# Layer 2 of a four-layer network: centring behind the relu's additions, one half's residual behind the next turn's factor products, one product instruction a half

## The chip, the cores and the metric

The kernel runs on one core of a Trainium2 chip. The metric is the time of one execution in microseconds (us) on the device. A core has five engines with a queue each, which run in order and wait for one another through semaphores: PE (TensorE, matrix products and transposes), DVE (VectorE), ACT (ScalarE), POOL (GpSimd) and SP (SyncE, which here issues every DMA). PE writes into PSUM[...].

## The reference, cut to what matters

Four layers are added to the image one after the other; each works on a group normalisation of its input. The change lies in the stretch in which the end of layer 1 and the whole of layer 2 are computed, with the first statistics of layer 3.

```
x = x + L1(gn(x))        # its last step: relu of a normalised product of the input and a factor per pixel
x = x + L2(gn(x))
x = x + L3(gn(x))

def L2(x):                                     # "involution", 3 x 3
    r  = relu(batchnorm(x @ Wr))               # 256 -> 64 channels
    w  = (r @ Ws).reshape(B, H, W, 16, 1, 9)   # nine weights for each of 16 groups, per pixel
    xi = x @ Wi                                # 256 -> 256
    patches = nine shifts of padded xi, stacked, reshaped to (B, H, W, 16, 16, 9)
    return sum(w * patches, axis=-1)
```

There are 16 images of 64 x 64 pixels and 256 channels, all in float32.

## The kernel before, in words

Layer 2 is the second of three blocks of the program. An image is cut into 8 chunks of 512 pixels. One loop of 151 turns does four jobs a turn, each on its own chunk, at distances given by `LAG`: `end` (the end of layer 1), 12 turns later `proj` (the projection xi of the same chunk), 20 turns later `inv` (the involution), and 30 turns later `cen` (the centring of the finished chunk for layer 3). In a steady turn the four jobs are in up to four images. The order of instructions on each engine is the order in which the code is written (`tc.manual_schedule()`).

The jobs, with their lines and the names of their tiles:

- `end_of_layer1` (L965) is a generator in three parts. First DVE makes `z` and `pf`, one for each half of the channels, from `x1` and the factors (L975). Then ACT applies the relu to both (L981) and POOL adds `x1`, which gives `x2` (L985). Last ACT squares `x2` for statistics (L992).
- `projected` (L1031): PE computes `px` for two halves, eight matmuls (L1038), ACT writes them into the padded image `pad` (L1042) and, at an image's last chunk, copies two edge columns (L1049, L1050).
- The involution needs `prepare` one turn ahead: `reduced2` gives `pr` and, through ACT, `rt` (L1059, L1062); `weights` gives `pw`, once for each half (L1069); `patches` transposes `pad` into `pt`, and ACT copies nine of them into `xs` (L1084, L1088). Then `products` (L1107) multiplies patches by weights on DVE, into `pd`, in four instructions a half, one for each row of pixels. Half 0 is summed over its nine taps on POOL (`sums_on_pool`, L1122 and L1123), half 1 on DVE (L1258). Both go into `x3`. `residual` (L1093) transposes `x2` into two PSUM tiles `lo`, and DVE adds one to each half of `x3` (L1261): half 1 first, then half 0, which has to wait for POOL.
- `turned` (L1125), a turn later, transposes `x3` into `c3`; `statistics3` (L1152) squares it. `stores` collects DMAs, which SP issues at the start of the next turn.
- `centred` (L1174): POOL subtracts the mean `gmb` from a loaded chunk `xc` (L880), and twelve DMAs write the result into `strips`.

Norms run beside this as generators, `norm2` and `norm3`: moments (L113 to L123), a matmul (`pg`), copies of the group mean (L140, and L142 for `ngm2`), the deviation (L146 to L148), a matmul (`pv`; with it `pb`, L864, in `norm3`), then `isq` (L93) and for `norm3` a copy of `pb` into `gmb` (L869). `norm2` ends with small matmuls `pm` (L1020) from which DVE makes `b2` and `bis` (L1026, L1028). Each call of `step()` moves every running norm by one part. A turn has three: one behind `turned` (before `projected`), one behind both products, and one at the end. A norm's first part (the moments) is run at the start of the turn after the statistics are complete.

A turn is called by r, its number modulo 8. In r=3 the next involution begins a new image, and `prepare` has to come behind `projected`, which writes the last chunk of that image; in all other turns it comes ahead of the relu. `norm3` computes its moments at r=5, its matmuls `pv` and `pb` and its `isq` at r=6. `norm2` computes its moments at r=0, `isq` at r=1, `bis` at r=3.

PSUM tiles: `pt`, `pr`, `px`, `pg`, `pv`, `pb` and `pm` all come from one pool, "tr", of three buffers. A new tile waits until the reader of the tile that had its buffer is done. Which of the three buffers a tile gets is settled when the program is built. `lo` has a pool of two buffers, `pw` one of three, `pd` and `xs` two each.

Of the kernel before, what the change touches and what calls it, by code (L numbers as in the profile page):

```python
# [11 lines left out]
ALU = mybir.AluOpType  # L12
# [3 lines left out]
P = 128  # L16
C = 256
# [19 lines left out]
def network(ctx: ExitStack, tc: tile.TileContext, a: dict, out: bass.AP):  # L37
    nc = tc.nc
# [59 lines left out]
    def step():  # L98

        for c in list(chains):  # L100
            if next(c, c) is c:
                chains.remove(c)
# [77 lines left out]
    with ExitStack() as st:  # L180
# [366 lines left out]
        def loads(n):  # L547
            for job in jobs(n):
                if job[0] == "q":
                    load("xn", job[1], job[3])  # L550
                else:
                    load(*job)
# [78 lines left out]
    with ExitStack() as st:  # L631
# [57 lines left out]
        for n in range(10):  # L689
            delta, c = n // 2, n % 2  # L690
# [28 lines left out]
        with tc.manual_schedule():  # L719
# [25 lines left out]
            for n, (ch, g) in enumerate(steps):  # L745
# [18 lines left out]
                b, k = g * 8, min(8, NI - g * 8)  # L764
# [134 lines left out]
    with ExitStack() as st:  # L899
# [45 lines left out]
        def taken(name):  # L945

            n = [k for k, _ in loaded].index(name)
            return loaded.pop(n)[1]
# [11 lines left out]
        def load_centred(i, rc):  # L960
            load("xc", [P, 4, C], *(
                (lambda t, k=k: t[:, k], src) for k, src in enumerate(centred_from(i, rc))
            ))

        def end_of_layer1(i, rc):  # L965

            if rc == 0:
                st0[i] = [
                    wk.tile([P, 2, NCH], F32, tag=f"st0{k}", name="st0") for k in range(2)
                ]  # L970
            sums, squares = st0[i]
            x1, pf = taken("x1"), taken("pf")
            zs = [wk.tile([P, 2, 256], F32, tag="z", name="z", bufs=1), pf]
            for h, z in enumerate(zs):
                nc.vector.scalar_tensor_tensor(  # L975
                    z, x1[:, h], ngm1[:, i, h : h + 1], pf, ALU.add, ALU.mult
                )
            yield
            x2 = wk.tile([P, 2, CT], F32, tag="x2", name="x2")
            for h, z in enumerate(zs):  # L980
                nc.scalar.activation(  # L981
                    z, z, AF.Relu, bias=bnp[:, 1, h : h + 1], scale=ab[:, 0, i, h : h + 1],
                    accum_out=sums[:, h, rc : rc + 1],
                )
                nc.gpsimd.tensor_tensor(  # L985
                    x2[:, h].rearrange("p (t g) -> p g t", g=2), z, x1[:, h], ALU.add
                )
            stores.append((x2_d[i, rc], x2))
            yield
            sq = wk.tile([P, CT], F32, tag="sq", name="sq", bufs=1)  # L990
            for h in range(2):
                nc.scalar.activation(  # L992
                    sq, x2[:, h], AF.Square,
                    bias=ngm1[:, i, h : h + 1], accum_out=squares[:, h, rc : rc + 1],
                )
            if rc == NCH - 1:
                begun.append(norm2(i))
# [104 lines left out]

        def products(oh, pw, xs):
            pd = pd_p.tile([P, 4, P, 9], F32, tag="pd", name="pd")
            for r in range(4):
                run = xs[:, r : r + 3].rearrange("p e j c -> p (e j c)")
                nc.vector.tensor_tensor(  # L1107
                    pd[:, r].rearrange("p (g f) k -> p g f k", f=16),
                    run[:, oh * 9 * P : (oh + 1) * 9 * P].rearrange(
                        "p (g f k) -> p g f k", f=16, k=9  # L1110
                    ),
                    pw[:, r].rearrange("p (g k) -> p g k", k=9).unsqueeze(2).broadcast_to(
                        [P, 8, 16, 9]
                    ),
                    ALU.mult,
                )
            return pd

        def sums_on_pool(pd, x3):
# [5 lines left out]
        def turned(i, rc, x3):  # L1125

            if rc == 0:
                st3[i] = [
                    wk.tile([P, 2, NCH], F32, tag=f"st3{k}", name="st3") for k in range(2)
                ]  # L1130
            c3 = wk.tile([P, 2, 2, 256], F32, tag="c3", name="c3", bufs=2)
            for oh in range(2):
                pt = tr.tile([P, 4, P], F32, tag="tr", name="pt")
                for r in range(4):
                    nc.tensor.transpose(pt[:, r, :], x3[:, r, oh * P : (oh + 1) * P], ident)
                nc.scalar.activation(  # L1136
                    c3[:, oh], pt.rearrange("p r t -> p (r t)").rearrange("p (t g) -> p g t", g=2),
                    AF.Copy, accum_out=st3[i][0][:, oh, rc : rc + 1],
                )
            x3n = x3_d[i].rearrange("(g r w) c -> g w r c", g=2, w=HW)  # L1140
            for g in range(2):
                stores.append((x3n[g][:, rc * 4 : rc * 4 + 4], x3[g:P:2]))
            for h in range(2):
                stores.append((
                    c3_d[i, :, h].rearrange("p (g t) -> p g t", g=2)[
                        :, :, rc * 256 : rc * 256 + 256
                    ],
                    c3[:, h],
                ))
            return c3  # L1150
# [23 lines left out]
        def centred(i, rc):  # L1174
            cen = wk.tile([P, 4, 4, 64], F32, tag="cen", name="cen")
            stores.extend(centred_strips(i, rc, taken("xc"), cen, gmb[i]))
# [6 lines left out]

        LAG = (0, 12, 20, 30)
        TURNS = NI * NCH + 23

        def jobs(n):

            at = [divmod(n - lag, NCH) for lag in LAG]
            return [
# [13 lines left out]
        with tc.manual_schedule():  # L1206
            loads(0)
            ahead, made = None, None
            for n in range(TURNS):
                end, proj, inv, cen = jobs(n)  # L1210
                nxt = jobs(n + 1)[2]
                done, stores[:] = list(stores), []
                loads(n + 1)
                for dst, src in done:
                    nc.sync.dma_start(out=dst, in_=src)
                nxt_cen = jobs(n + 1)[3]
                if nxt_cen:
                    load_centred(*nxt_cen)
                now, ahead = ahead, None
                for c in begun:  # L1220
                    next(c)
                chains.extend(begun)
                begun.clear()
                ending = end_of_layer1(*end) if end else None
                if ending:
                    next(ending)
                if inv:
                    w1 = weights(now[1], 1)
                    x3 = wk.tile([P, 4, C], F32, tag="x3", name="x3", bufs=3)

                def prepare():
                    x2r, rt = reduced2(*nxt)
                    ahead = [x2r, rt]
                    ahead.append(patches(*nxt, lambda: ahead.append(weights(rt, 0))))
                    return ahead

                if nxt and nxt[1]:
                    ahead = prepare()
                if ending:
                    next(ending)  # L1240
                if inv:
                    los = residual(now[0])
                c3 = turned(*made) if made else None
                step()
                if proj:
                    projected(*proj)
                if inv:
                    pd = products(0, now[2], now[3])
                    sums_on_pool(pd, x3)
                if nxt and not nxt[1]:  # L1250
                    ahead = prepare()
                if inv:
                    pd1 = products(1, w1, now[3])
                step()
                if made:
                    statistics3(*made[:2], c3)
                if inv:
                    nc.vector.tensor_reduce(x3[:, :, P:C], pd1, AX.X, ALU.add)  # L1258
                    for oh in (1, 0):
                        half = x3[:, :, oh * P : (oh + 1) * P]  # L1260
                        nc.vector.tensor_tensor(half, half, los[oh], ALU.add)  # L1261
                step()
                if ending:
                    next(ending, None)
                made = (*inv, x3) if inv else None
                if cen:
                    centred(*cen)
            for dst, src in stores:
                nc.sync.dma_start(out=dst, in_=src)

# [2 lines left out]
    with ExitStack() as st:  # L1273
# [203 lines left out]
        for n, (i, quarter, t) in enumerate(turns):  # L1477
# [41 lines left out]
            if n % gap == 2 and n // gap < NCH:  # L1519
                cen = wk.tile([P, 4, 4, 64], F32, tag="xw", name="cen", bufs=6)  # L1520
# [3 lines left out]
            if n in features:  # L1524
                tp, k = features[n]
# [124 lines left out]
```

## Time and profile before

| | |
|---|---|
| time, median of 3 runs | 8560.48 us (8559.8 to 8580.07) |
| the profiled execution: time, span | 8603.53 us, 8601.7 us |
| layer 2's products, first to last start | 3634.3 to 6178.6 us |
| DVE busy from 4100 to 5834 us | 1638 of 1734 us |
| POOL, ACT, PE busy in the same stretch | 1253, 1075 and 1311 us |
| DMA engines busy in the same stretch | 0.71 of 16 engines, 233 GB/s |

The profile's page lists the busy time of each engine, its share in 40 equal slices of the span, and groups of instructions by source line with their number, busy time, mean duration in ns, and the idle time just before them with what ended it. The timeline gives single instructions in order: start, duration, engine, line, operation, output<-inputs, and in brackets the idle time before and its end. A mean over a group can hide two kinds of turn, and a busy engine can be stalled inside an instruction.

### The profile page before, as it was taken

To read this page: it belongs to the slowest core of one execution; us is meant where nothing else is said; L and a number is where in the kernel's file an instruction comes from. 1 tells how busy PE (TensorE), PEld (TensorE's weight loads), DVE (VectorE), ACT (ScalarE), POOL (GpSimd) and SP (SyncE) were. 2 spreads that over 40 slices of the span, in tenths; PEclk is the share of its full clock that TensorE was granted. 3 is DMA by queue.
4 is the path that set the end of the run, shared out by engine and by line. 5 is a ranking of instruction groups with operands and counts; after the bars stand their busy time and mean duration, and the time that the engine had idled before them with its cause. 6 is when DMAs were issued, how large, how long until landed. Compare 5 with 4: busy or idle time off the path is not lost. (4 is left out here: it accounts for less than half of the span.)

```text
span 8601.7 us, 215728 instructions
## 1 busy us (share of the span) xinstructions
PE 6924.3 (80%) x88348; PEld 5146.2 (60%) x88348; DVE 6022.7 (70%) x7839; ACT 4835.8 (56%) x11136; POOL 3054.3 (36%) x2154
## 2 busy tenths in 40 slices
PE   7888888888888776477777777778588888888888
PEld 5666666666666542254555555555376767777776
DVE  6777777777766757499999999999744444444444
ACT  3555555555555536666666656665355555555554
POOL 1222222222222200367777777777611112111112
PEclk9999999999999868799888888889799999999999
DMA  6543333443333327756767677676578878888887
GB/s 221 180 141 133 133 128 133 142 137 130 130 113 108 101 80 244 234 188 230 241 230 239 229 232 236 228 240 195 173 222 257 248 243 255 252 258 252 252 256 241
DMA packets 1081775, 1695.70 MB, mean 197 GB/s; under 512 B 138834, under 2 KB 684963, under 8 KB 1079635
## 3 DMA queue, kind: packets, MB, share of 16 engines
q1 hardware_dynamic: 1080786, 1681.90, 60.7%
q8 instruction: 696, 11.40, 0.6%
q14 instruction: 293, 2.39, 0.1%
HBM read 1234.54 MB, written 469.76 MB: 198 GB/s over the span
## 5 line engine op out<-in xcount | busy, mean ns | idle before, releaser
L1107 DVE TENSOR_TENSOR pd<-xs,pw 128x1152 f32<-128x1152 f32 x1024 | 1305.3, 1346 | 5.3 <-ACT xs L1088 5.3
L1367 PE MATMUL pk<-rt,span 64*128 64x176 f32 x12288 | 1179.9, 328 | 51.3 <-issue 44.9
L1122 POOL TENSOR_TENSOR pd<-pd 128x2048 f32<-128x2048 f32 (+2 forms) x384 | 1066.8, 2778 | 314.6 <-DVE pd L1107 294.5
L1377 ACT ACTIVATE wm<-pk,spanb 128x176 f32<-128x176 f32 x2560 | 847.0, 425 | 554.8 <-PE pk L1367 551.5
L1453 POOL TENSOR_TENSOR ex<-ex,rx 128x192 f32<-128x192 f32 (+2 forms) x768 | 436.3, 571 | 1855.3 <-DVE ex L1446 1152.3
L1367 PEld LDWEIGHTS pk<-rt,span 64*128 64x128 f32 x12288 | 969.4, 191 | 128.2 <-issue 69.8
L292 PE MATMUL pkv<-wq,xn 128*128 128x256 f32 x4096 | 1000.8, 390 | 49.4 <-DVE isq L93 27.6
L1446 DVE SCALAR_TENSOR_TENSOR ex<-pa,msk,ex 128x192 f32<-128x192 f32 x704 | 294.0, 418 | 1056.9 <-ACT ex L1445 984.2
L292 PEld LDWEIGHTS pkv<-wq,xn 128*128 128x128 f32 x4096 | 792.2, 196 | 280.5 <-issue 154.0
L375 POOL TENSOR_TENSOR qa<-qa,mq 128x1024 f32<-128x1024 f32 x256 | 493.7, 1950 | 1295.0 <-DVE mq L387 633.8
L1433 PE MATMUL pa<-wm,xw 126*32 126x48 f32 x45056 | 762.9, 214 | 221.7 <-issue 179.8
L1382 DVE TENSOR_TENSOR wm<-pk,spanb 128x704 f32<-128x704 f32 x896 | 793.8, 888 | 187.6 <-PE pk L1367 185.7
L1433 PEld LDWEIGHTS pa<-wm,xw 126*32 126x32 f32 x45056 | 626.7, 111 | 411.5 <-issue 332.8
L1038 PE MATMUL px<-x2p,wis 128*128 128x512 f32 x1024 | 581.7, 717 | 196.1 <-ACT c L1136 130.2
L1084 PE MATMUL pt<-ident,pad 128*128 128x128 f32 x4608 | 613.6, 287 | 129.0 <-ACT rt L1062 76.4
L1084 PEld LDWEIGHTS pt<-ident,pad 128*128 128x128 f32 x4608 | 522.8, 147 | 287.9 <-ACT rt L1062 97.2
L1088 ACT COPY xs<-pt 128x512 f32<-128x512 f32 x1152 | 591.4, 601 | 138.5 <-PE pt L1084 129.8
L1258 DVE TENSOR_REDUCE x<-pd 128x512 f32<-128x4608 f32 x128 | 633.4, 4948 | 1.9
L280 PE MATMUL pq<-xn,wq 128*128 128x512 f32 x1024 | 525.3, 629 | 29.0 <-ACT xn L165 22.6
L424 PE MATMUL py<-wo,o 128*128 128x256 f32 x2048 | 533.0, 409 | 4.2 <-DVE maps L510 1.9
L1445 ACT ACTIVATE ex<-pa,msk 128x192 f32<-128x192 f32 x704 | 299.8, 426 | 413.0 <-PE pa L1433 219.4
L424 PEld LDWEIGHTS py<-wo,o 128*128 128x128 f32 x2048 | 488.2, 309 | 30.3 <-issue 5.6
(233 smaller groups left out, 11870.8 us busy)
## 6 DMA issues: line engine op xcount, KB each, us to landing
xw<-strips SPq DMA_DIRECT2D x1408, 256.0 KB
xn<-in_x SPq DMA_DIRECT2D x256, 512.0 KB
x_d<-x SPq DMA_DIRECT2D x256, 512.0 KB
xin<-in_x SPq DMA_DIRECT2D x128, 512.0 KB
x<-in_x SPq DMA_DIRECT2D x128, 512.0 KB
xm<-x_d SPq DMA_DIRECT2D x128, 512.0 KB
x<-x_d SPq DMA_DIRECT2D x128, 512.0 KB
x<-x_d SPq DMA_DIRECT2D x256, 256.0 KB
```

Of the source, the lines that this page charges most:

```text
L292: nc.tensor.matmul(pkv[:, q], lhsT=xn[:, h, q * P : (q + 1) * P], rhs=wq[:, h, f0 + P : f0 + 384], start=(h == 0), stop=(h == 1),)
L424: nc.tensor.matmul(py[:, q, :], lhsT=om[i, hf][:, :, ch * 4 + q], rhs=wo[:, hf, :], start=(hf == 0), stop=(hf == 1),)
L1038: nc.tensor.matmul(px, lhsT=w[:, h, fh * P : (fh + 1) * P], rhs=x2[:, h], start=(h == 0), stop=(h == 1),)
L1084: nc.tensor.transpose(pt[:, k, h * P : (h + 1) * P], lines[:, h, rc * 4 + e + k, 2 * j : 2 * j + P], ident,)
L1088: nc.scalar.copy(xs[:, e : e + 2, j, :], pt)
L1107: nc.vector.tensor_tensor(pd[:, r].rearrange("p (g f) k -> p g f k", f=16), run[:, oh * 9 * P : (oh + 1) * 9 * P].rearrange("p (g f k) -> ...
L1122: nc.gpsimd.tensor_tensor(pd[..., 0:n], pd[..., 0:n], pd[..., n : 2 * n], ALU.add)
L1258: nc.vector.tensor_reduce(x3[:, :, P:C], pd1, AX.X, ALU.add)
L1367: nc.tensor.matmul(pkv[:, b, m], lhsT=span[half, first + gg, s0 : s0 + P], rhs=rto[half, o // 4 * 2 + m, :], start=True, stop=True,)
L1377: nc.scalar.activation(dst[:, m // 2, m % 2], pkv[:, m // 2, m % 2], AF.Identity, bias=spanb[:, g0 + m : g0 + m + 1],)
L1382: nc.vector.tensor_tensor(dst, pkv, spanb[:, g0 : g0 + 4].rearrange("p (b m) -> p b m", b=2).unsqueeze(3).broadcast_to([P, 2, 2, NTL]), AL ...
L1433: nc.tensor.matmul(pav[p0 : p0 + 32, :, tj * TC : (tj + 1) * TC].rearrange("c g (w v) -> c g w v", v=2), lhsT=xw[0:TILE_IN, k, tj, 32 * q ...
```

## The change

Three things are changed, all in the loop of layer 2.

1. `products` is one DVE instruction a half, over all four rows, with a hand-written access pattern that steps by one row of patches (3*C elements).
2. Within a turn, DVE makes `z` and `pf` first. Then come one `step()`, the first part of a norm that has just begun, and the residual addition of half 0 of the turn before (`made` now carries the tile `los[0]`). The `step()` at the turn's end is the one that has moved. The addition of half 1 stays behind its reduction.
3. `centred` is called behind the second part of `end_of_layer1`, that is behind the relu's additions on POOL and ahead of the sums, and its distance is 31 turns. Its twelve DMAs come ahead of those of `turned` in the list of stores.

```diff
         def products(oh, pw, xs):
             pd = pd_p.tile([P, 4, P, 9], F32, tag="pd", name="pd")
-            for r in range(4):
-                run = xs[:, r : r + 3].rearrange("p e j c -> p (e j c)")
-                nc.vector.tensor_tensor(
-                    pd[:, r].rearrange("p (g f) k -> p g f k", f=16),
...
+            run = xs.rearrange("p e j c -> p (e j c)")[:, oh * 9 * P : (oh + 1) * 9 * P]
+            run = bass.AP(run.tensor, run.offset, [run.ap[0], [3 * C, 4], [9 * 16, 8], [9, 16], [1, 9]])
+            nc.vector.tensor_tensor(
+                pd.rearrange("p r (g f) k -> p r g f k", f=16),
+                run,
+                pw.rearrange("p r (g k) -> p r g k", k=9).unsqueeze(3).broadcast_to(
+                    [P, 4, 8, 16, 9]
+                ),
+                ALU.mult,
+            )
             return pd
...
-        LAG = (0, 12, 20, 30)
+        LAG = (0, 12, 20, 31)
...
                 now, ahead = ahead, None
+                ending = end_of_layer1(*end) if end else None
+                if ending:
+                    next(ending)
+                step()
                 for c in begun:
                     next(c)
                 chains.extend(begun)
                 begun.clear()
-                ending = end_of_layer1(*end) if end else None
-                if ending:
-                    next(ending)
+                if made:
+                    half = made[2][:, :, 0:P]
+                    nc.vector.tensor_tensor(half, half, made[3], ALU.add)
                 if inv:
                     w1 = weights(now[1], 1)
...
                 if ending:
                     next(ending)
+                if cen:
+                    centred(*cen)
                 if inv:
                     los = residual(now[0])
-                c3 = turned(*made) if made else None
+                c3 = turned(*made[:3]) if made else None
                 step()
...
                 if inv:
                     nc.vector.tensor_reduce(x3[:, :, P:C], pd1, AX.X, ALU.add)
-                    for oh in (1, 0):
-                        half = x3[:, :, oh * P : (oh + 1) * P]
-                        nc.vector.tensor_tensor(half, half, los[oh], ALU.add)
-                step()
+                    half = x3[:, :, P:C]
+                    nc.vector.tensor_tensor(half, half, los[1], ALU.add)
                 if ending:
                     next(ending, None)
-                made = (*inv, x3) if inv else None
-                if cen:
-                    centred(*cen)
+                made = (*inv, x3, los[0]) if inv else None
```

More of the change, by code (lines that the diff above doesn't have):

```diff
@@ L1104, in products @@
             pd = pd_p.tile([P, 4, P, 9], F32, tag="pd", name="pd")
-            for r in range(4):
-                run = xs[:, r : r + 3].rearrange("p e j c -> p (e j c)")
-                nc.vector.tensor_tensor(
-                    pd[:, r].rearrange("p (g f) k -> p g f k", f=16),
[L1109 to L1116, printed above, removed]
+            run = xs.rearrange("p e j c -> p (e j c)")[:, oh * 9 * P : (oh + 1) * 9 * P]
[8 more added lines that the diff above has]
+            )
             return pd
```

## The prediction

> **What bounds the kernel now.** I read the page's slices, then the waits of VectorE inside layer 2, then the timelines of the four engines over two turns. A turn is named by r, its number modulo 8, and P_r is the start of its first product; POOL is GpSimd, ACT ScalarE, PE TensorE.
>
> ```profile
> DVE  6777777777766757499999999999744444444444
> L1107 DVE TENSOR_TENSOR pd<-xs,pw 128x1152 f32<-128x1152 f32 x1024 | 1305.3, 1346 | 5.3 <-ACT xs L1088 5.3
> L1258 DVE TENSOR_REDUCE x<-pd 128x512 f32<-128x4608 f32 x128 | 633.4, 4948 | 1.9
> ```
>
> Layer 2 is the run of nines, from 3634 to 6184 us. Busy VectorE is not the whole story: here are the turns r=6 and r=7 of one image, VectorE, then POOL, then PE, then ACT.
>
> ```profile
> 5142.18 10.19 DVE L1107 TENSOR_TENSOR pd<-xs,pw 128x1152 f32<-128x1152 f32 x8
> 5152.29 0.15 DVE L93 TENSOR_SCALAR isq<-pv 128x2 f32<-128x2 f32 x1
> 5152.69 4.94 DVE L1258 TENSOR_REDUCE x<-pd 128x512 f32<-128x4608 f32 x1
> 5157.66 1.28 DVE L1261 TENSOR_TENSOR x<-x,lo 128x512 f32<-128x512 f32 x2
> 5158.87 2.30 DVE L975 SCALAR_TENSOR_TENSOR z<-x,ngm,pf 128x512 f32<-128x512 f32 x1
> 5161.21 0.75 DVE L975 SCALAR_TENSOR_TENSOR pf<-x,ngm,pf 128x512 f32<-128x512 f32 x1
> ...
> 5179.59 0.69 DVE L1261 TENSOR_TENSOR x<-x,lo 128x512 f32<-128x512 f32 x1 [1.74 <-POOL x L1123]
> ...
> 5158.26 2.36 POOL L880 TENSOR_TENSOR cen<-xc,gmb 128x1024 f32<-128x1024 f32 x1
> 5166.78 1.28 POOL L985 TENSOR_TENSOR x<-z,x 128x512 f32<-128x512 f32 x1 [6.16 <-DMA c_d<-c]
> ...
> 5169.26 8.55 POOL L1122 TENSOR_TENSOR pd<-pd 128x2048 f32<-128x2048 f32 x3
> 5177.88 1.68 POOL L1123 TENSOR_TENSOR x<-pd 128x512 f32<-128x512 f32 x1
> ...
> 5144.41 1.98 PE L1038 MATMUL px<-x2p,wis 128*128 128x512 f32 x4
> 5152.49 3.60 PE L1038 MATMUL px<-x2p,wis 128*128 128x512 f32 x4 [6.10 <-DVE isq L93]
> ...
> 5165.74 0.87 ACT L981 ACTIVATE z<-z,bnp,ab 128x512 f32<-128x512 f32 x1
> ```
>
> Two limits are to be seen. An ordinary turn (r=7 ends one, 19 to 19.8 us) is VectorE's own queue, with one stall in it: z takes 2.30 us instead of 0.75 because the centring holds POOL until 5160.6. The other limit is a chain across engines: the second px waits 6.10 us for isq, a norm link that VectorE reaches only behind its products; ACT then runs in order through the second pad, four squares and the next patches, so the relu of z starts at 5165.74 although z was there at 5161.2; the additions, the sums and the residual follow, and the next products start at 5183.98: 41.80 us for two turns. The late-patch pair (r=3, 4) has the same form, from 5077.47 to 5122.37, 44.90 us. An image takes 165.4 us (1654.4 us for the ten from the reduce of turn 42 to that of turn 122).
>
> [...] four px matmuls took 1.98 us warm, 3.60 us after 6.1 us of idling. [...]
>
> **The change, part by part.**
> *One product a half.* Eight products start 10.12 us apart as a group, 1.265 us each[...]. One instruction becomes 4.87 us start to start (the reduce over the same 4608 elements takes 4.95), 0.39 us less a turn. Bounds: nothing, if each row of the access costs what an instruction does, to 0.5 us.
> *z and pf first, half 0 after, centring behind the additions.* VectorE's turn is then 9.73 (products) + 4.98 (reduce) + 0.6 (half 1) + 1.45 (z, pf) + 0.67 (half 0) = 17.45 us, against 19.0 to 19.8. z starts 15.4 us after P, the sums end near 15.2, so it seldom meets a busy POOL; where it does, it waits for one POOL instruction. Links between pf and half 0 cost 0.55 us (deviation) in two turns. Half 0 now stands in front of the products and waits there for the sums; behind it on VectorE is the whole turn, and on PE the second lo and the transposes of x3, so that c comes some 0.6 us later, up to 0.4 us a turn where PE is slow. The centring falls into the 2.46 us that POOL idles before its sums in an ordinary turn: nothing. Where the relu is late, POOL has no idle there and it is paid in full, 2.34 us, in front of the sums. So the late chain becomes, from the relu of z to the next products: 1.04 + 2.48 (additions) + 2.34 + 10.30 (sums) + 0.63 (half 0) = 16.8 us, where before it was 14.5 us and then z, pf and links (18.24 us in the lines above).
> *SP's queue.* Strips (12 DMAs, 8.7 us) now stand before the x3 and c3 stores; their producers are turns old, and loads remain some 20 us ahead of use (pf issued at 5074.1 for z at 5094.0). Nothing, with 3 us per image as the far bound.
> *What the diff does not show.* The built order with its waits says it: the PSUM buffers of "tr" rotate differently. Before, px waits for a VectorE link in r=6 alone (its second). After, from turn 43 on, it does so in five turns of eight: r=0, second px, for ngm2; r=1, first px, for isq; r=3, first px, for bis; r=5, second, for the copy of gm; r=6, pb ahead of both, for isq. All these links stand behind both products on VectorE, near P+9.95 (5152.44 less 5142.18, less 0.39). Before, the buffers gave these waits to transposes that came later anyway. Behind the px wait pads, squares, pw, pr, rt, patches, the relu.
> From the second px to the relu: 13.25 us in the lines above, 14.93 in the image before (4985.79 to 5000.72); mean 14.1. With both px behind the link 1.9 more, 16.0.
> So for two turns: r=0 and r=5, 9.95+14.1+16.8 = 40.9; r=1, 42.7; r=6, 43.3 (0.6 for pb). For r=3: px at 10.2, eight cold matmuls 5.4, second pad and edge copies to 17.1, pr to 17.5; then 16.2 us before from first transpose (5088.06) to relu (5104.23), less 1.3 for a warm array: relu at 32.4, next but one products at 49.2, 49.7 with the links of r=5; its own patches are done at 23.4, so r=3 alone takes 23.5.
> An image: r=3 to r=5 49.7; r=5 to r=6 18.2 (17.45, links, a lock); r=6 to r=0 43.3; r=0 to r=1 18.2; r=1 to r=3 42.7. Sum 172.1, against 165.4: 6.7 us slower.
>
> **Sum**, against the profiled execution (span 8601.7 us, time 8603.5; the median of the runs is 8560.5, 0.5% lower, so shares of a per cent carry over). Turns 20 to 42, where the rotation is still the old one: 0.4 off each of eight, about 2 off each late pair, 1.4 to 2.3 off the twelve with centring, less 0.3 each where the patches arrive late: -24. Turns 43 to 122: ten images, +67. Turns 123 to 127, one pair more: +8. The last 20 turns, with no z and no pf: 0.45 each and a shorter first one, -11. Sum +40: 8600 us.
>
> **Rivals.**
> *Warm array, so not slower.* If the array stays at full rate through the waits, eight px take 3.6 us instead of 5.4 in r=3, and r=6 and r=1 shorten likewise: 172.1-5.4 = 166.7 an image, +13 in ten, +3, -24, -11: 8541 us; it decides below 168.4 us an image (ten images then give back the -24, +5 and -11). For it: px runs at 1.98 us for four where PE was busy. Against: 3.60 us after 6 us of idling, 5.40 for eight after 3.2.
> *VectorE alone.* If the px waits are hidden, the late pairs come to their present relu less 0.39 plus 16.8, 43.1 and 40.0 us, and the other four turns to 17.8: 154 us an image, 11 us off each of ten: 8405 us. Against it: r=6 shows the wait unhidden.
> *SP paces.* It issues 27 DMAs a turn in about 20.2 us (strips of one turn at 5059.22, of the next at 5079.39); if nothing else binds, 162 us an image: 8490 us.
> *Worse pile-up.* Slow clock throughout (as in the image before, 14.93) on all five, and z and links locked out by the sums' instructions: 179 us an image, 8670 us.
>
> **How the numbers follow.** Forecast 0.62, warm 0.13, VectorE 0.06, SP 0.07, pile-up 0.12. Time 8600. The forecast's own range is 8570 to 8640 (2 us an image either way, the product's bounds). With the rivals: 8500 to 8665. Within 0.3%, 25.7 us, is what a measurement of this kernel can tell from no change. Slower: 0.52 of the forecast's 0.62 and the pile-up, 0.64; within: 0.10 and half the warm case, 0.17; faster: the rest, 0.19.
>
> **What would show it.** Right: 256 products of about 4.95 us; z at 0.75; in the waits, px for bis, ngm2, gm, isq, 6 to 8 us each and some fifty in all; turns of about 23.5, 26, 18, 23, 20.5, 18, 22.5, 20 from r=3. Wrong: an image under 169 us with these waits present, or the waits absent. A product over 5.1 us refutes the first part.

## The result, and the profile after

The changed kernel takes 8689.74 us (median of four runs, 8683.08 to 8703.29); the kernel before, run beside it, 8570.27 us. The ratio is 1.0141, 95% interval 1.012 to 1.0163: slower by 1.4%, 119 us. The profiled execution after has a span of 8681.2 us and a time of 8683.08 us. From the first product of layer 2 to the first of its last turn went 2535.5 us before and 2651.0 after: 115 us, so the loss is layer 2's. (The rest of these two profiled executions differs by 36 us the other way: that of the kernel before, 8603.5 us, was longer than any of its runs in this comparison.)

From the page of the changed kernel: VectorE's row of slices, the products and the reduce (count, busy time, mean ns of one, idle time before them and what ended it).

```profile
DVE  6777777777777757599999999999934444444444
L1107 DVE TENSOR_TENSOR pd<-xs,pw 128x4608 f32<-128x4608 f32 x256 | 1255.9, 4947 | 68.7 <-ACT xs L1088 68.7
L1262 DVE TENSOR_REDUCE x<-pd 128x512 f32<-128x4608 f32 x128 | 633.4, 4948 | 1.9
```

The products are done as the change says: 256 instead of 1024, 49 us less busy (1305.3 before). But VectorE now waits 68.7 us for `xs`, where it waited 5.3: the patches come late. Why they do is in the waits of PE. Here are those of `px` and `pb` in the changed kernel, between 4240 and 5860 us, some nine images (total us, number of waits, longest), and below them the one such wait that the kernel before has.

```profile
PE px L1038 <- issue: 51.8, 10, 5.2
PE px L1038 <- DVE ngm L142: 41.0, 9, 4.6
PE px L1038 <- DVE gm L140: 36.5, 9, 4.1
PE px L1038 <- DVE isq L93: 32.2, 9, 3.9
PE pb L864 <- DVE isq L93: 19.2, 9, 2.2
...
PE px L1038 <- DVE isq L93: 54.7, 10, 6.1
```

Five kinds, once an image each, 4 to 5 us a piece for `px`. The ten put down to "issue" are the r=3 ones: px follows directly on `bis`, the link that had its buffer. In the kernel before, the only one is `isq` in r=6. Here are `bis` and px in one r=3, and px in an r=7, where PE had not waited.

```profile
5136.78 0.14 DVE L1028 TENSOR_TENSOR bis<-bi,pm 128x2 f32<-128x2 f32 x1
...
5137.02 6.26 PE L1038 MATMUL px<-x2p,wis 128*128 128x512 f32 x8 [5.18 <-issue]
...
5222.79 3.60 PE L1038 MATMUL px<-x2p,wis 128*128 128x512 f32 x8
```

The second thing to be seen is the boundary from r=7 to r=0, VectorE and then GpSimd (start, duration, instruction), where the products of r=7 had started at 5220.25.

```profile
5235.76 0.95 DVE L975 SCALAR_TENSOR_TENSOR z<-x,ngm,pf 128x512 f32<-128x512 f32 x1
5236.74 2.00 DVE L975 SCALAR_TENSOR_TENSOR pf<-x,ngm,pf 128x512 f32<-128x512 f32 x1
5238.67 0.15 DVE L113 TENSOR_REDUCE mom<-st 128x2 f32<-128x16 f32 x1
5238.75 0.15 DVE L114 TENSOR_REDUCE mom<-st 128x2 f32<-128x16 f32 x1
5238.86 1.03 DVE L118 SCALAR_TENSOR_TENSOR gn_mv<-mom,mean 128x2 f32<-128x2 f32 x1
5239.92 1.19 DVE L121 TENSOR_TENSOR mom<-gn_mv,ngm 128x2 f32<-128x2 f32 x1
5241.14 2.26 DVE L122 TENSOR_TENSOR mom<-mom 128x2 f32<-128x2 f32 x1
5243.44 0.16 DVE L123 SCALAR_TENSOR_TENSOR gn_mv<-mom 128x2 f32<-128x2 f32 x1
5243.52 0.68 DVE L1228 TENSOR_TENSOR x<-x,lo 128x512 f32<-128x512 f32 x1
5244.12 9.81 DVE L1107 TENSOR_TENSOR pd<-xs,pw 128x4608 f32<-128x4608 f32 x2
...
5236.24 1.96 POOL L1121 TENSOR_TENSOR x<-pd 128x512 f32<-128x512 f32 x1
5238.16 1.71 POOL L985 TENSOR_TENSOR x<-z,x 128x512 f32<-128x512 f32 x1
5239.83 1.26 POOL L985 TENSOR_TENSOR x<-pf,x 128x512 f32<-128x512 f32 x1
5241.05 2.33 POOL L880 TENSOR_TENSOR cen<-xc,gmb 128x1024 f32<-128x1024 f32 x1
```

The sums are complete at 5238.20. Half 0 (L1228) needs nothing more, but it starts at 5243.52, 5.3 us later, because pf and the links (the small VectorE instructions of a norm, here norm2's moments) stand in front of it. Its patches were ready: the last of them left ScalarE at 5236.2. GpSimd goes straight from x into two additions and the centring, which end at 5238.20, 5239.87, 5241.09 and 5243.38; pf ends half a microsecond behind the first of these, L118, L121 and L122 within 0.02 us of the other three. So each of these four gets in at one seam between two GpSimd instructions, or is locked out, as it is called below; the two reductions L113 and L114 are not held up. L122 works on 128x2 elements and takes 2.26 us; in the kernel before it takes 0.161.

The turns, means over the last seven whole images (turns 67 to 122), in us. The first image with the new rotation took 172.3 us.

```
r          3      4      5      6      7      0      1      2    image
before   19.12  25.42  19.81  19.69  23.02  19.80  19.78  18.99  165.6
forecast 23.5   26     18     23     20.5   18     22.5   20     172.1
after    23.69  27.86  17.94  23.86  23.91  17.96  22.28  20.00  177.5
```

### The profile page after: what moved, and what is told of

Same layout as the page of the kernel before. It is cut to its first block, busy times and chain, and to the rows that moved or that the text cites. A ratio compares the mean times of both kernels' runs of the same rounds, so it can differ in the third digit from the quotient of the medians.

```text
span 8681.2 us, 214953 instructions
## 1 busy us (share of the span) xinstructions
PE 6949.9 (80%) x88348; PEld 5175.8 (60%) x88348; DVE 6102.1 (70%) x7071; ACT 4829.3 (56%) x11136; POOL 3089.1 (36%) x2154
## 5 line engine op out<-in xcount | busy, mean ns | idle before, releaser
L1107 DVE TENSOR_TENSOR pd<-xs,pw 128x4608 f32<-128x4608 f32 x256 | 1255.9, 4947 | 68.7 <-ACT xs L1088 68.7
L1120 POOL TENSOR_TENSOR pd<-pd 128x2048 f32<-128x2048 f32 (+2 forms) x384 | 1090.4, 2839 | 231.2 <-DVE pd L1107 211.0
L1038 PE MATMUL px<-x2p,wis 128*128 128x512 f32 x1024 | 604.1, 739 | 186.1 <-issue 51.8
L1084 PE MATMUL pt<-ident,pad 128*128 128x128 f32 x4608 | 592.8, 280 | 86.8 <-ACT rt L1062 86.8
L1084 PEld LDWEIGHTS pt<-ident,pad 128*128 128x128 f32 x4608 | 500.4, 143 | 248.8 <-ACT rt L1062 109.2
```

Of the source, the lines that this page charges most:

```text
L1038: nc.tensor.matmul(px, lhsT=w[:, h, fh * P : (fh + 1) * P], rhs=x2[:, h], start=(h == 0), stop=(h == 1),)
L1084: nc.tensor.transpose(pt[:, k, h * P : (h + 1) * P], lines[:, h, rc * 4 + e + k, 2 * j : 2 * j + P], ident,)
L1107: nc.vector.tensor_tensor(pd.rearrange("p r (g f) k -> p r g f k", f=16), run, pw.rearrange("p r (g k) -> p r g k", k=9).unsqueeze(3).broa ...
L1120: nc.gpsimd.tensor_tensor(pd[..., 0:n], pd[..., 0:n], pd[..., n : 2 * n], ALU.add)
```

## The experiments

Theory A: the slowdown comes from px waiting for VectorE links, a side effect of how the "tr" buffers rotate in the built program. Theory B: what goes beyond the forecast is the links locked out between pf and half 0. Rivals: SP's order of stores, the centring in the late chains, the merged product. Each comparison was with the kernel before on the same chip, so ratios are compared, not times; its median there lay between 8545 and 8584 us. What each gave, with the length of an image (mean of the same seven) and of turns 20 to 42, from each run's profiled execution:

```
                          us       ratio, 95% interval       image  turns 20-42
before (own profile)                                         165.6  451.1
the changed kernel        8689.74  1.0141 [1.012, 1.0163]    177.5  444.6
x1_strips_behind          8516.71  0.9963 [0.9952, 0.9973]   162.5  440.2
x2_links_first            8626.39  1.0089 [1.0053, 1.0124]   174.1  434.2
x3_merge_alone            8530.20  0.9985 [0.9973, 0.9997]   163.8  449.3
x4_centring_alone         8649.97  1.0123 [1.0086, 1.016]    177.5  436.9
y1_centring_rot_kept      8551.44  0.9969 [0.9959, 0.998]    163.9  437.0
y2_c3_by_act              8721.42  1.0180 [1.0165, 1.0195]   180.6  445.3
y3_c3_act_links_first     8682.25  1.0129 [1.0114, 1.0144]   178.7  434.6
y4_after_c3_by_act        8690.53  1.0143 [1.0128, 1.0158]   179.7  446.0
z1_one_store_behind       8676.18  1.0143 [1.0126, 1.016]    177.5  443.9
z2_pf_one_load            8506.22  0.9942 [0.9925, 0.996]    161.0  442.9
z3_x1_links_first         8515.37  0.9957 [0.9941, 0.9973]   162.1  437.2
z4_no_centring_move       8605.88  1.0051 [1.0034, 1.0069]   168.3  461.7
w1_centring_and_merge     8552.57  0.9971 [0.9959, 0.9984]   163.8  437.5
w2_centring_merge_pf      8551.17  0.9963 [0.9952, 0.9973]   163.8  432.8
```

**The px waits: x1 and z1.** In x1 the centring is called a little further down:

```diff
-                if cen:
-                    centred(*cen)
                 if inv:
                     los = residual(now[0])
                 c3 = turned(*made[:3]) if made else None
+                if cen:
+                    centred(*cen)
```

> The changed kernel with the call of the centring moved behind turned(): every engine's own order stays, only SP issues the strips behind the x3 and c3 stores; in the built order no px then waits for a VectorE link (the waits fall on transposes). Theory A (px waits are most of the loss): px waits gone from the trace, the image 177.4 us falls to some 160 (late pairs 43.1 and 40.0, the other four turns 17.8, plus 1.7 and 4.5 us for locked-out links), ten images 174 us less: about 8510 us. Theory B (links locked out between pf and half 0 are most of it): the px waits go, but the image stays above 172 us, over 8640 us. SP as pacer: image at 162 us or more with loads late.

The ratio is 0.9963 and the image 162.5 us: the whole loss is gone and a gain of 0.4% in its place. In x1's waits of PE (same stretch) px waits for no VectorE link:

```profile
PE px L1038 <- ACT pad L1042: 7.8, 10, 0.8
...
PE px L1038 <- ACT c L1134: 1.7, 7, 0.3
```

x1 differs from the changed kernel in SP's order too. z1 takes that rival away. It is x1 with one c3 store issued behind the strips; every other engine has exactly x1's instructions in x1's order, but the buffers rotate as in the changed kernel.

```diff
-            stores.extend(centred_strips(i, rc, taken("xc"), cen, gmb[i]))
+            stores[-1:-1] = centred_strips(i, rc, taken("xc"), cen, gmb[i])
```

> x1 with one thing changed: the last of a turn's two c3 stores is issued behind the strips. PE, VectorE, ScalarE and GpSimd have exactly x1's order of instructions; in the built order the tr buffers rotate as in the changed kernel (px waits for bis, gm, ngm2 and isq, pb for isq). Theory A (the px waits are the loss): as the changed kernel, image 177 us, 1.2 to 1.6% slower than before. Rival (x1 gained by the order of strips and stores on SP): within 0.3% of x1, some 0.997 of before.

1.0143, image 177.5 us, the changed kernel's own figures. Its waits of PE:

```profile
PE px L1038 <- issue: 51.9, 10, 5.2
PE px L1038 <- DVE ngm L142: 40.8, 9, 4.6
PE px L1038 <- DVE gm L140: 36.3, 9, 4.1
PE px L1038 <- DVE isq L93: 30.3, 9, 3.9
PE pb L864 <- DVE isq L93: 19.0, 9, 2.1
```

z1 and the changed kernel differ in the place of three stores on SP and agree; z1 and x1 differ in the place of one, which took a median of 0.56 us to issue in the changed kernel, and lie 15 us an image apart. What goes with the 15 us is the waits. Theory A holds: the px waits are worth 1.8%. That the place of a store on SP changes them shows in these lists; by which step it changes the buffer that a PSUM tile gets stays open.

**The links: x2.** The changed kernel with the links ahead of z and pf:

```diff
+                step()
+                for c in begun:
+                    next(c)
+                chains.extend(begun)
+                begun.clear()
                 ending = end_of_layer1(*end) if end else None
                 if ending:
                     next(ending)
-                step()
-                for c in begun:
-                    next(c)
-                chains.extend(begun)
-                begun.clear()
```

> The changed kernel with the norm links (step and begun) ahead of z and pf rather than behind them. The px waits stay where they are (r=6 gets one for gmb in place of pb's). Theory B: the 4 to 5 us at r=7 to 0 and some 1.7 at r=4 to 5 go, and about as much in the early turns: 6 us an image, 60 to 75 us in all, 8620 us. Rival (the links only fill time in which half 0 would wait anyway, or z late by the links costs as much): within 20 us of 8690.

Layer 2 went from 2651.0 to 2604.6 us, 46 less, against the 60 to 75 expected: 10.4 in turns 20 to 42 and 3.4 an image. r=6 and r=7 together fell from 47.77 to 44.33 us. The same boundary in x2, VectorE and GpSimd:

```profile
5195.49 1.22 DVE L122 TENSOR_TENSOR mom<-mom 128x2 f32<-128x2 f32 x1
5196.75 0.16 DVE L123 SCALAR_TENSOR_TENSOR gn_mv<-mom 128x2 f32<-128x2 f32 x1
5196.96 1.99 DVE L975 SCALAR_TENSOR_TENSOR z<-x,ngm,pf 128x512 f32<-128x512 f32 x1
5198.99 0.75 DVE L975 SCALAR_TENSOR_TENSOR pf<-x,ngm,pf 128x512 f32<-128x512 f32 x1
5199.66 0.68 DVE L1228 TENSOR_TENSOR x<-x,lo 128x512 f32<-128x512 f32 x1
...
5188.16 8.54 POOL L1120 TENSOR_TENSOR pd<-pd 128x2048 f32<-128x2048 f32 x3
5196.78 1.63 POOL L1121 TENSOR_TENSOR x<-pd 128x512 f32<-128x512 f32 x1
5199.97 1.28 POOL L985 TENSOR_TENSOR x<-z,x 128x512 f32<-128x512 f32 x1 [1.57 <-ACT z L981]
```

The links now meet the end of the sums, which half 0 waits for anyway; the sums end at 5198.41 and half 0 starts 1.3 us later. And as z comes behind them, GpSimd has no additions to do until 5199.97. So theory B is right in kind and in sign. The delay of half 0 behind its sums fell by 4.8 us an image (5.32 to 1.25 at r=7 to 0, 1.16 to 0.47 at r=4 to 5). Of that 3.4 us came through: counted from the start of r=6, the sums of r=7 end 0.6 us later, where px starts at P+10.95 instead of P+10.5, and r=1 and r=2 take 0.4 us more.

**The merged product: x3.** Only `products` of the changed kernel, in the kernel before.

> The kernel before with one product instruction a half and nothing else. px waits stay as before (r=6 alone), waits of transposes of x3 for links become waits of pr. Theory: 0.39 us off each of 128 turns, 40 to 50 us: 8520 us. Rival (pr now waits for links behind the products, and the next patches with it): no gain or a loss, 8560 us or more.

0.9985: a gain, 15 us by the medians, a third of what its own instructions save (0.39 us a turn, 50 us in 128 turns). Both ends of the expectation were partly right. `pr` now waits for links, at 2.0 to 3.6 us:

```profile
PE pr L1059 <- DVE isq L93: 32.0, 9, 3.6
...
PE pr L1059 <- DVE gm L140: 20.3, 10, 2.0
...
PE pr L1059 <- DVE ngm L142: 18.9, 9, 2.1
```

**The centring: x4, y1.** The kernel before with the centring behind the additions and lag 31 and nothing else; in y1 the call stands behind `turned()`, in x4 two lines earlier.

> The kernel before with the centring behind the additions (and its lag 31) and nothing else. In the built order px then waits for links in r=3, 6, 0 and 1, behind both products. Theory A: slower than before, image 165.4 to some 178 us (late relu plus 2.34 centring plus the old 18.24 us chain in two more turns), about 8690 us. Rival (the move is what it says[...]): 1.55 us off each of 80 turns, 8450 us.

> The kernel before with the centring behind the additions, as in x4, but called behind turned(): in the built order the tr buffers then rotate as in the kernel before (px waits for a link in r=6 alone). Theory A: the 12 us an image that x4 lost were the px waits: image 162 to 165, about 8520 us. Rival (the centring itself in the late chains, 2.34 us in front of the sums, and POOL's order cost x4 its time): image 175 us or more, about 8640 us.

1.0123 and 0.9969, images of 177.5 and 163.9 us: again the same edit with and without the px waits. x4, then y1:

```profile
PE px L1038 <- DVE ngm L142: 87.1, 9, 10.1
PE px L1038 <- DVE isq L93: 68.4, 18, 6.2
PE px L1038 <- issue: 62.2, 9, 8.1
```

```profile
PE px L1038 <- DVE isq L93: 58.0, 10, 6.1
```

In y1 the centring's own effects can be read: r=5, 6, 0 and 1 fall to 18.46, 18.24, 18.47 and 17.87 us, as z takes 0.748 us on the mean instead of 1.452; the late turns r=4 and r=7 rise to 28.13 and 25.37, since there the centring stands in front of the sums. The rest is 1.7 us an image.

**The deferral: z4, w1.** z4 is the changed kernel with the centring back at the turn's end and lag 30.

> The changed kernel without the centring's move (back at the turn's end, lag 30): one product a half and the deferred half 0 and links alone. No px waits for a link. z meets the centring again, so VectorE's turn is 17.45 plus 1.55, 19 us, but the late chains carry no centring. Theory A: faster than before, image 161 to 164, ratio 0.993 to 0.998. Rival (the deferral of half 0 and the links is what costs): 1.005 or more.

The forecast failed: 1.0051, image 168.3, turns 20 to 42 at 461.7 us, with no px wait for a link. The fair comparison is with x3, which lacks the deferral alone: 0.9985, image 163.8 us. Around one boundary of z4 (r=5 to 6), VectorE and then GpSimd:

```profile
4992.42 2.81 DVE L975 SCALAR_TENSOR_TENSOR z<-x,ngm,pf 128x512 f32<-128x512 f32 x1
...
4996.32 1.21 DVE L148 TENSOR_TENSOR gn_d<-gn_d,gn_mv 128x2 f32<-128x2 f32 x1
4997.46 0.68 DVE L1228 TENSOR_TENSOR x<-x,lo 128x512 f32<-128x512 f32 x1
...
4992.33 2.35 POOL L880 TENSOR_TENSOR cen<-xc,gmb 128x1024 f32<-128x1024 f32 x1
...
5003.14 8.53 POOL L1120 TENSOR_TENSOR pd<-pd 128x2048 f32<-128x2048 f32 x3 [4.39 <-DVE pd L1107]
```

z, the deviation and half 0 all queue ahead of the products. z takes 2.81 us beside the centring, where pf behind it takes 0.75, and the deviation's L148 1.21 us beside an addition, where L147 takes 0.16; then GpSimd idles 4.39 us for the product. So the deferral is a loss where GpSimd works at the boundary. w1 leaves it out and keeps the other two parts:

> The kernel before with the centring behind the additions (called behind turned()) and one product a half, without the deferral of half 0 and the links. px waits as in the kernel before. If the deferral is a loss in itself (links and z meet GpSimd): below x1, image 161 us, some 8500 us, ratio 0.994 to 0.996. If it is a gain that x1 needs: above y1 less 0.39 a turn, ratio 0.997 or more. The other way to read x1: it and y1 stand at the same 162 to 164 us an image because SP and the DMAs pace both; then within 0.2% of both.

w1 gave 0.9971, as y1, and x1 0.9963; the intervals overlap, layer 2 took 2496.9 us in w1 and 2484.3 in x1. With the centring out of its way the deferral came out as neither a loss nor much of a gain. The two are not parted by it alone, though: w1 keeps the px wait for `isq` in r=6 (55.6 us in ten), which x1 does not have. The merge on top of y1 gave 0.1 us an image: r=5, 6, 0 and 1 fell by 0.4 us each, r=2, r=7 and r=3 took it back.

**What holds x1 at 162 us: z2, z3, w2, y2, y3, y4.** In x1 SP issues 27 DMAs a turn. The expectations read its queue as full; the issues themselves take 16.5 of the 20.3 us of a turn, and the rest is short gaps. Loads do come late: `pr` waits 29.4 us for x2r in nine images.

> x1 with the factor row pf loaded in one DMA rather than two, the same bytes. In x1 SP issues without a pause, 20.3 us a turn. If SP's issuing paces x1: 0.6 to 0.7 us a turn less, image 157 to 158, about 50 us below x1. Rival (the DMA's bytes or VectorE pace it): within 10 us of x1.

> x1 with the norm links ahead of z and pf; in the built order the second px then waits for isq in r=6, as in the kernel before. Theory B alone: 10 us less in turns 20 to 42 and 3 us less an image, 40 us below x1. If SP paces an image already: only the early turns gain, 10 us or nothing; the px wait of r=6 may take 2 us an image back.

> w1 with the factor row loaded in one DMA, as in z2. If the transfers pace w1: another 10 to 15 us as from x1 to z2. If VectorE and the late chains pace it: the same as w1 within 5 us.

z3 equals x1, as expected if something other than the links paces it. z2 gave 1.5 us an image, not 5, though pf's issues fell from 1.34 to 0.77 us a turn: the sum of all SP's issues stayed at 16.4 us a turn (16.49 in x1), the others having become longer. w2 equals w1. So neither the count of DMAs alone nor the links hold these kernels at 161 to 164 us; that the bytes do (236 GB/s in x1's stretch, 232 in the kernel before's) is not shown. Nor need one thing hold them all: in that stretch of 1620 us VectorE is busy, lock-outs included, for 1588 us in x1 and for 1413 in w1. z2 is the fastest kernel of the study, though its interval overlaps x1's.

To relieve SP in another way, y2 let ScalarE issue the two c3 stores:

```diff
-                stores.append((
-                    c3_d[i, :, h].rearrange("p (g t) -> p g t", g=2)[
+                nc.scalar.dma_start(
+                    out=c3_d[i, :, h].rearrange("p (g t) -> p g t", g=2)[
                         :, :, rc * 256 : rc * 256 + 256
                     ],
-                    c3[:, h],
-                ))
+                    in_=c3[:, h],
+                )
```

> x1 (no px waits) with the two c3 stores of a turn issued by ScalarE behind its own copies rather than by SP. In x1 SP issues 27 DMAs back to back, 20.3 us a turn, and an image of eight turns takes 162.5. If SP now paces: 1.5 to 2 us less of SP a turn, image 157 to 158, about 8460 us, and the centring no longer waits for xc. Rival (VectorE's lock-outs and the late pairs pace, SP has slack): within 15 us of x1's 8517; or slower, by ScalarE's two issues in the late chains.

> y2 with the norm links ahead of z and pf; px waits for no link here either. Theory B: the same 3 to 4 us an image as from the changed kernel to x2: 30 to 45 us below y2, about 8425 us. Rival (without the px waits half 0 waits for no locked-out link): the same as y2.

> The changed kernel with the c3 stores by ScalarE and the centring where it is: SP still issues the strips ahead of the x3 stores, but no px waits for a link in the built order. Theory A: as y2, about 8460 us, since the order of strips and x3 stores on SP is worth nothing. Rival (x1 gained by SP's order, the strips behind the stores): 8600 us or more.

All three were far off: 1.018, 1.0129, 1.0143. In y2's waits of SP (total us, number, longest) its loads and stores wait for the transfers that ScalarE issued, 285 us in nine images, and x1's list has no such wait:

```profile
SPq L942 <- DMA c_d<-c: 205.4, 50, 7.2
SPq L1213 <- DMA c_d<-c: 79.9, 42, 6.6
```

Loads then land late: `pr` waits 127.8 us for x2r, 29.4 in x1. y4 thus says nothing on SP's order; z1 does. Between y2 and y3 the links show once more: 10.7 us in turns 20 to 42, 1.9 an image.

## Why the prediction was wrong, step by step

*Products.* Forecast 4.87 to 4.95 us each and 0.39 us less a turn; measured 4.947 each, 9.81 us for two together (4.86 from start to start), and 49 us less in 128 turns. Right. The 4.87 was the author's estimate; what an instruction costs beside its elements no run shows by itself.

*px waits.* Right in place and in kind, all five, and shown to be the cause by x1 against z1. px starts at P+10.16 in r=3, 10.48 in r=6 and 9.94 in r=1 (10.2, 10.55 and 9.95 forecast). "6 to 8 us each" was too long: 4 to 5, as PE comes to px later. "Turns of about 23.5, 26, 18, 23, 20.5, 18, 22.5, 20" holds within 0.9 us in six of eight.

*The late chain.* From the relu of z to the end of the sums, 16.2 us were forecast; r=4 has 16.7. The sums end at P+49.8 in r=3 (48.6 forecast), P+41.8 in r=6 (42.7), P+41.6 in r=1 (42.1). Nearly right, and no net miss.

*The step that failed* is "Links between pf and half 0 cost 0.55 us (deviation) in two turns" and "z starts 15.4 us after P, the sums end near 15.2, so it seldom meets a busy POOL; where it does, it waits for one POOL instruction". That was worked out for an ordinary turn and carried to the late ones. In a late turn the sums end long after VectorE is done, so pf and the moments run into x, additions and centring, one instruction each. The prediction allowed for such a hold-up in z, which the trace of the kernel before shows (2.30 us against 0.75), and not in the small links: at the boundary above L122 took 2.26 us, against 0.161, and ended 0.02 us behind the centring. The kernel before already showed what a link can cost: the first link of each norm's moments behind the reductions met the centring there and took 1.5 us, where the later ones, with no GpSimd instruction beside them, took 0.16.

```profile
L116 DVE TENSOR_SCALAR gn_mv<-mom 128x2 f32<-128x2 f32 x10 | 15.1, 1511 | 0.0
L118 DVE SCALAR_TENSOR_TENSOR gn_mv<-mom,mean 128x2 f32<-128x2 f32 x10 | 15.0, 1500 | 0.0
```

Half 0 starts 5.3 us after its sums at r=7 to 0, where the sum had nothing for links, and 1.16 at r=4 to 5, where it had 0.5. That is 6.0 us an image more than forecast; less 0.2 in the chains and 0.5 in the two ordinary turns (17.94 and 17.96 against 18.2), it is, within 0.2, the 5.4 us that the image missed (177.5 against 172.1). So of +116 us in turns 43 to 122 against +67, pf and the links are the difference by the trace. x2, which moves the links, gave back 34 of these 49 us; that all 49 are theirs is not shown by a run.

*Turns 20 to 42.* "-24" was -6.5. x2 has -17 there: 10.4 of the 17.5 us missed are the same links; the other 7 stay open.

*Turns 123 to 127.* "+8" was +8.9. Right.

*The last 20 turns.* "-11" was -2.9, and x2 does not change it (-3.2). z1, with the deferral, has -7.0; w1, without it, -11.8; and w2, which there differs from w1 in nothing, as the loads of pf are over, -8.1. So executions of like code lie 4 us apart there, and the cause of the missing 8 us stays open.

In all, layer 2 missed the forecast by 75 us: 49 in the ten images, 17.5 in the early turns, 8 in the last and 1 in between. 46 of them came back in x2.

*SP's queue and centring.* Strips ahead of the stores cost nothing in themselves: z1 and the changed kernel differ in that order and agree. What they did do is set the rotation. "The centring ... is paid in full in the late chain" is confirmed by y1.

*Rivals.* "Warm array" was wrong in r=3: eight px took 6.26 us, longer even than the 5.4 us forecast, against 3.60 where PE had not waited; the granted clock was 0.59 over the first eight and 1.00 over the others. "Warm" and "cold" are clocks that the trace of the kernel before shows as well: four px took 1.98 us at 1.00, and 3.60 at 0.55 behind the wait of 6.10; eight took 5.40 at 0.68 behind one of 3.22 (at 4295.07). The "1.3 for a warm array" came near: the twelve transposes at 5088.06 took 2.79 us at 0.50 in the kernel before, those at 5145.07 in the changed kernel 1.59 at 1.00. "Worse pile-up" named "z and links locked out by the sums' instructions", and gave 179 us an image against 177.5 measured. Its number is near partly by luck. It also had a slow clock on all five waits, as from 4985.79 to 5000.72 in the kernel before (granted 0.68, against 0.88 in the 13.25 us of the image after), but the chains of r=6 and r=1 ended 0.9 and 0.5 us earlier than forecast; and the links met the additions and the centring rather than the sums. "VectorE alone" gave 154 us an image if the px waits were hidden; x1, which has none of them, stays at 162.5. "SP paces" gave 162 us an image, where x1 came to rest, but z2 did not show SP's issuing to be the reason.

## What to carry to other kernels

When a reordering makes a kernel slower, look first at which waits the built program has, not at which the code suggests: here one store's place on a DMA queue changed the buffers that PSUM tiles got, and with them 1.8% of the time, while the order of instructions on every other engine stayed the same. Keep small links of this kind out of the stretch in which GpSimd works without a pause in front of something that the next turn waits for; price each at the GpSimd instruction that it may meet, here up to 2.26 us for L122, not at its own 0.16 us. And price a boundary for the late turns apart from the ordinary ones: what runs behind a late GpSimd meets other work, and here half 0 started 5.3 us behind its sums at r=7 to 0.

## What the runs showed of the hardware

A VectorE instruction on 128x2 elements (L122) took 0.161 us in the kernel before, where none of the 20 in this stretch overlapped a GpSimd instruction, and 1.872 us on the mean in the changed kernel, as these rows show, before and then after:

```profile
L122 DVE TENSOR_TENSOR mom<-mom 128x2 f32<-128x2 f32 x20 | 3.2, 161 | 0.7
```

```profile
L122 DVE TENSOR_TENSOR mom<-mom 128x2 f32<-128x2 f32 x18 | 33.7, 1872 | 0.6
```

Where GpSimd worked without a pause, from 5236.24 to 5243.38, pf and three links each got in at one seam: they took 2.00, 1.03, 1.19 and 2.26 us and ended 0.54, 0.02, 0.02 and 0.02 us behind four GpSimd instructions. Two reductions onto 128x2 elements (L113, L114) took 0.15 us each within the same run. And in y2 SP waited 285 us in nine images for the two stores a turn that ScalarE issued there; in the changed kernel, where SP issues them itself, one took a median of 0.56 us to issue.
